# Transformer stack with self and cross attention on one core: query and key transfers issued per round instead of from one ordered queue

## The chip, the cores and the metric

The kernel runs on one core of a Trainium2 chip. The time is device microseconds (us) of one execution; the median of several executions counts. The engines are TensorE (PE: matrix products and, as PEld, loads of their stationary operand), VectorE (DVE), ScalarE (ACT), GpSimd (POOL) and SyncE (SP), whose queue issues nearly all DMA transfers here.

## The reference

Two layers; each has self attention, cross attention to a context of 1,601 rows, and a gated feed-forward part. There are 4 batches of 512 rows of width 320, and 20 heads of width 16.

```python
def _attn(x, ctx, wq, wk, wv, wo, bo, heads):
    ...
    sim = jnp.einsum('bhid,bhjd->bhij', q, k) * scale
    a = jax.nn.softmax(sim, axis=-1)
    out = jnp.einsum('bhij,bhjd->bhid', a, v)
    out = out.transpose(0, 2, 1, 3).reshape(b, n, heads * dh)
    return out @ wo + bo
...
h1 = _ln(x, n1_g, n1_b)
x = _attn(h1, h1, q1, k1, v1, o1_w, o1_b, heads) + x
h2 = _ln(x, n2_g, n2_b)
x = _attn(h2, context, q2, k2, v2, o2_w, o2_b, heads) + x
h3 = _ln(x, n3_g, n3_b)
proj = h3 @ ff_w1 + ff_b1
a, g = jnp.split(proj, 2, axis=-1)
ff = a * jax.nn.gelu(g, approximate=False) @ ff_w2 + ff_b2
return ff + x
```

## The kernel before

**Units.** Attention is cut into units of one batch and four heads: 20 self units, then 20 cross units, then four feed-forward units (one a batch), and the same for layer 1. The units are numbered through: 0 to 19 self, 20 to 39 cross, 40 to 43 feed-forward, 44 on for layer 1. A self unit has 4 chunks of 128 keys, a cross unit 13. The four heads lie in four strips of 32 rows, so that products of four heads can run on PE side by side.

**One chunk** (`main`, from L1117). For each head PE forms the scores `st` from keys and queries (L1128: two products with the two halves of the split queries, and a third with `nrows` and `ones`, which takes the row maximum off). ACT takes the exponentials (L1138), PE multiplies them with the values into `av` (L1152, one chunk late), ACT copies that to `vo` (L1168) and POOL adds it to `o` (L1169). Two *rounds* are counted a chunk.

**Pair products.** The row maxima of a coming unit are needed before its scores. They come from products `sps` of two heads each (L936), which DVE reduces to `nmax` or `pm` (L953). A self unit has 8 of them, a cross unit 26. `giver` (L1380) hands one a round to the chunk in hand, if a unit among the next two (or the first cross unit, which is marked early) has its data *at hand*, that is, three rounds after its reads were issued (`at_hand`, L1363). What is then still missing one round before the maxima are due is given as a lump behind the chunk's scores. Two chunks before a unit starts, `max_end` (L1000) splits and turns its maxima on DVE and sends them to the rows `nrows` by eight transfers (L1015) from SP.

**Queries and keys.** `add_proj` (L648) puts a unit's projections into the scheduler's chains: for a self unit `both` (L721 on PE, L737 on ACT, the split into `high` and `low` on POOL at L645), for a cross unit `keys_of_context` (L787) and `queries` (L759). The results go to DRAM (`kway`, `qway`, two buffers of each) and come back in another layout to `kT` and `q`. Each such step is a *move*, issued from SP at L690. A self unit has five: write the keys (2 transfers), write the queries (3), read the keys (1), read the two halves of the queries (1 and 1). A cross unit has eight. A unit's read waits for the unit three before it, whose buffers it takes (`unread`, `free`).

**The order.** `steps` (L400) runs once a chunk and picks, from the heads of the chains, the one that is due first; each step has a cost and a due round, and a running credit says how much may be done. The moves stand in a chain of their own, "slots", in the order in which the units were added; only its head may go, one move a round (`add_moves`, L819), and two rounds after the last move of its unit. If a unit is wanted whose moves have not all gone, `at_once` (L1367) issues them, with its projections if these are missing, on the spot.

Of the kernel before, what the change touches and what calls it, by code (L numbers as in the profile page):

```python
# [65 lines left out]
def kernel(ctx: ExitStack, tc: tile.TileContext, x, context, ws, out):  # L66
# [264 lines left out]
    chains = {n: deque() for n in ("divide", "project", "slots", "norm", "context", "early", "proj", "values")}  # L331
    clock = {"round": 0, "credit": 0.0, "lights": 0, "slots": 0, "tiles": None}
# [67 lines left out]
    def steps(beside, lights=1):  # L400


        tick()
        clock["lights"], clock["slots"] = lights, 1
# [233 lines left out]
    pending = {"q": 0, "k": 0}  # L638

    def by_rows(t):  # L640
        return t.rearrange("j h d n -> j (h d) n")
# [6 lines left out]
    def add_proj(u):  # L648
        chain = "early" if u.early else "proj"

        due = lead(u) - 9
# [30 lines left out]
        def move(pairs, then=None, what=None, may=yes):  # L682
# [13 lines left out]
            u.moves.append((f, yes if what else may))  # L696
            u.moving = clock["round"]

# [16 lines left out]
        def both(part):  # L715
# [29 lines left out]
            move([(to_q[:, 0], high[:GD]), (to_q[:, 1], low[:GD]), (to_q[:, 2], high[:GD])], what="q")  # L745
            move([(u.kT[:, u.k0 : u.k0 + N].bitcast(F32), by_rows(to_k))], may=free)
            read_queries(to_q)
# [31 lines left out]
        def keys_of_context():  # L779
# [27 lines left out]
            move([(full[:, :, i * HALF : (i + 1) * HALF], of[:, i, :, :HALF]) for i in range(2)], may=free)  # L807
            move([(to[:, 4 * QT :].rearrange("p (a w) -> p a w", a=4), of[:, 1, :, HALF:])], may=free)
# [10 lines left out]
        def add_moves(n, due):  # L819
            for _ in range(n):  # L820
                add(
                    "slots", 0.0, lambda: u.moves and u.moves.popleft()[0](), due,
                    lambda: u.moves[0][1]() if u.moves else u.when is not None,
                    lambda: clock["slots"] > 0 and clock["round"] >= u.moving + 2,
                )

        if not u.cross:
            for part in range(2):
                add(chain, (0.46,) * 3, lambda part=part: both(part), due - 2 + 2 * part, lambda part=part: part or way_free("q") and way_free("k"))
            add_moves(5, due)  # L830
        else:
            add(chain, 2.45, keys_of_context, keys_due, lambda: way_free("k"))
            add_moves(4, keys_due)
# [3 lines left out]
            add_moves(4, due)  # L837
# [378 lines left out]
    def add_norms(i):  # L1216

        while norms and norms[0].i <= i + (1 if norms[0].kind == "ff" else AHEAD + 1 if norms[0].early else 6):
# [3 lines left out]
            else:  # L1222
# [4 lines left out]
                due = lead(u) - 10  # L1227
# [139 lines left out]
    def at_once(v):  # L1367
# [7 lines left out]
        while v.moves:  # L1375
            f, may = v.moves.popleft()
            assert may()
            f()
# [97 lines left out]

    for i, u in enumerate(units):
# [44 lines left out]
```

## Time and profile before

| | |
|---|---|
| median of three executions | 4405.97 us (4396.28 to 4408.82) |
| profiled execution | 4397.83 us |
| its span, first to last instruction | 4396.0 us |
| mean granted clock of PE | 0.819 |
| PE busy | 3874.0 us (88%) |
| DVE, ACT, POOL busy | 2104.9, 1973.4, 1124.2 us |
| DMA, mean over the span | 51 GB/s |

An engine's busy time is the union of its instructions. The granted clock is the share of full speed at which PE was let run; at 0.5 every product takes twice its time. A row of the timeline gives start, length, engine, source line, operation, output <- inputs, shapes and a count of instructions merged; in brackets stands the idle time before it and what ended it. A row of a group gives busy time and mean ns of one, and after the bar the idle time before it. A row of waits gives the total, the number and the longest.

By the count of values products the stages of the profiled execution end at about 705 us (self, layer 0), 1960 us (cross, layer 0), 2296 us (feed-forward, and the first self unit of layer 1), 2908 us (self, layer 1), 4116 us (cross, layer 1).

### The profile page before, as it was taken

To read this page: it belongs to the slowest core of one execution; us is meant where nothing else is said; L and a number is where in the kernel's file an instruction comes from. 1 tells how busy PE (TensorE), PEld (TensorE's weight loads), DVE (VectorE), ACT (ScalarE), POOL (GpSimd) and SP (SyncE) were. 2 spreads that over 40 slices of the span, in tenths; PEclk is the share of its full clock that TensorE was granted. 3 is DMA by queue.
4 is the path that set the end of the run, shared out by engine and by line. 5 is a ranking of instruction groups with operands and counts; after the bars stand their busy time and mean duration, and the time that the engine had idled before them with its cause. 6 is when DMAs were issued, how large, how long until landed. Compare 5 with 4: busy or idle time off the path is not lost.

```text
span 4396.0 us, 82324 instructions
## 1 busy us (share of the span) xinstructions
PE 3874.0 (88%) x34290; PEld 1896.2 (43%) x34290; DVE 2104.9 (48%) x3113; ACT 1973.4 (45%) x3909; POOL 1124.2 (26%) x1222
## 2 busy tenths in 40 slices
PE   6778778899899999999988787788999899999999
PEld 3334344334434444545543333343344345445455
DVE  4434452524527776762234344535146376767321
ACT  2334334244255776771123333342443577777411
POOL 2222122122233344330111222221222344443200
PEclk7787687557678998999996877775577899999999
DMA  2221111110112122120012212111101121211100
GB/s 83 75 73 60 61 53 31 46 51 24 50 52 72 58 65 81 58 57 4 14 37 73 67 44 65 52 30 34 46 28 43 53 83 61 67 56 52 50 11 12
DMA packets 202224, 223.24 MB, mean 51 GB/s; under 512 B 63760, under 2 KB 143772, under 8 KB 201852
## 3 DMA queue, kind: packets, MB, share of 16 engines
q1 hardware_dynamic: 201468, 217.59, 16.4%
q8 instruction: 269, 4.41, 0.4%
q14 instruction: 103, 0.84, 0.1%
q10 hardware_dynamic: 176, 0.27, 0.0%
q0 software_dynamic: 208, 0.14, 0.0%
HBM read 119.55 MB, written 86.58 MB: 47 GB/s over the span
## 4 chain that ended last, share of the span: by engine, by line
PE 60%; DVE 14%; DMA 11%; ACT 5%; SPq 4%; issue 2%; POOL 2%; POOLq 0%; DVEq 0%; ACTq 0%
PE st L1128 19%; PE av L1152 16%; DVE pm L953 9%; PE fps L1258 6%; ACT pr L1138 4%; DMA qway<-high 4%; PE yps L1312 4%; DVE nmax L953 3%; DMA q<-qway 3%; DMA kway<-stages 3%; PE sps L936 3%; PE ops L1062 2%; PE kps L787 2%; PE vps L878 2%; SPq L690 2%
## 5 line engine op out<-in xcount | busy, mean ns | idle before, releaser
L1138 ACT ACTIVATE pr<-st 128x512 f32<-128x512 f32 (+1 forms) x2720 | 1404.2, 603 | 1098.2 <-PE st L1128 1052.5
L1169 POOL TENSOR_TENSOR o<-o,vo 128x512 f32<-128x512 f32 x576 | 736.3, 1278 | 2161.8 <-ACT vo L1168 2154.0
L1128 PE MATMUL st<-q,kT 32*128 32x512 f32 (+1 forms) x5440 | 1127.7, 523 | 142.9 <-ACT low L737 63.1
L953 DVE TENSOR_REDUCE pm<-sps 128x2 f32<-128x1024 f32 (+1 forms) x1142 | 1134.5, 1047 | 245.3 <-PE sps L936 211.9
L936 PE MATMUL sps<-kT,q 32*128 32x512 f32 x5120 | 1022.6, 547 | 194.5 <-DMA q<-qway 117.8
L1152 PE MATMUL av<-pr,vals 128*32 128x512 f32 (+1 forms) x5440 | 890.6, 727 | 122.2 <-ACT pr L1138 120.2
L1128 PEld LDWEIGHTS st<-q,kT 32*128 32x128 f32 (+1 forms) x5440 | 509.1, 207 | 885.9 <-ACT pr L1138 456.9
L936 PEld LDWEIGHTS sps<-kT,q 32*128 32x128 f32 x5120 | 460.8, 223 | 477.3 <-DVE pm L953 179.3
L953 DVE TENSOR_REDUCE nmax<-sps 128x1 f32<-128x512 f32 (+1 forms) x459 | 381.7, 894 | 565.9 <-PE sps L936 556.6
L1128 PE MATMUL st<-nrows,ones 2*128 2x512 f32 (+1 forms) x2720 | 603.9, 456 | 29.3 <-DMA nrows<-turned 26.6
L1168 ACT COPY vo<-av 128x512 f32<-128x512 f32 x576 | 347.1, 603 | 143.8 <-PE av L1152 141.7
L1128 PEld LDWEIGHTS st<-nrows,ones 2*128 2x128 f32 (+1 forms) x2720 | 329.5, 215 | 73.7 <-issue 24.0
L1152 PEld LDWEIGHTS av<-pr,vals 128*32 128x32 f32 (+1 forms) x5440 | 118.3, 116 | 436.0 <-ACT pr L1138 423.0
L1258 PE MATMUL fps<-hT,w 128*128 128x512 f32 x640 | 284.3, 597 | 0.6 <-DVE hid L1282 0.6
L1281 ACT ACTIVATE gl<-fps,b 128x512 f32<-128x512 f32 x80 | 50.6, 683 | 391.6 <-PE fps L1271 274.0
L1032 DVE STREAM_TRANSPOSE oturn<-o 128x512 f32<-128x512 f32 x80 | 56.3, 704 | 272.2 <-POOL o L1169 272.1
L1258 PEld LDWEIGHTS fps<-hT,w 128*128 128x128 f32 x640 | 118.8, 190 | 148.9 <-issue 144.0
L1282 DVE SCALAR_TENSOR_TENSOR hid<-fps,b,gl 128x512 f32<-128x512 f32 x80 | 56.4, 747 | 263.0 <-ACT gl L1281 263.0
L1312 PE MATMUL yps<-w,hid 128*128 128x320 f32 x640 | 175.3, 434 | 1.3 <-DVE nmax L953 1.3
L645 POOL CAST high<-low 128x256 fp32r<-128x256 f32 (+1 forms) x79 | 39.6, 501 | 491.0 <-ACT low L737 314.8
L1312 PEld LDWEIGHTS yps<-w,hid 128*128 128x128 f32 x640 | 120.7, 190 | 56.9 <-issue 6.1
L737 ACT ACTIVATE low<-qkps,scales 128x256 f32<-128x256 f32 x78 | 35.2, 472 | 243.9 <-DMA qway<-low 132.6
(86 smaller groups left out, 2560.0 us busy)
## 6 DMA issues: line engine op xcount, KB each, us to landing
q<-qway SPq DMA_DIRECT2D x160, 256.0 KB
kway<-stages SPq DMA_DIRECT2D x160, 224.0 KB
kT<-kway SPq DMA_DIRECT2D x80, 384.0 KB
kT<-kway SPq DMA_DIRECT2D x40, 256.0 KB
aT<-o SPq DMA_DIRECT2D x320, 32.0 KB
qway<-high SPq DMA_DIRECT2D x160, 64.0 KB
nrows<-turned SPq DMA_DIRECT2D x636, 2.0 KB
qway<-high SPq DMA_DIRECT2D x79, 128.0 KB
```

What stands on the lines that cost most here:

```text
L690: queue.dma_start(out=to, in_=of)
L787: nc.tensor.matmul(ps[i * GD : (i + 1) * GD, :w], lhsT=wk_q[rows, k, u.g * GD : (u.g + 1) * GD], rhs=first.kvT[rows, k, i * HALF : i * HAL ...
L878: nc.tensor.matmul(ps[:, :w], lhsT=u.kvT[rows, k, s * P : (s + 1) * P], rhs=wv_q[rows, k, h0 * DH : h1 * DH], start=(k == 0), stop=(k == K ...
L936: nc.tensor.matmul(ps, lhsT=u.q[j * SLOT : (j + 1) * SLOT, e, t * P : (t + 1) * P], rhs=u.kT[j * SLOT : (j + 1) * SLOT, u.k0 + s * 512 : u ...
L953: nc.vector.tensor_reduce(to[:, j : j + n], part, AX.X, ALU.max, negate=(ns == 1))
L1128: nc.tensor.matmul(st[:r, :], lhsT=ones[rows.start : rows.start + 2, :r] if e == 2 else u.keys(rows, c), rhs=u.rows[rows.start : rows.star ...
L1138: nc.scalar.activation(p[:r], st[:r], AF.Exp)
L1152: nc.tensor.matmul(ps[j * SLOT : (j + 1) * SLOT, :], lhsT=columns_of[:r, head : head + SLOT], rhs=pr.pop((c, j))[:r, :], start=True, stop= ...
L1168: nc.scalar.copy(vo, ps)
L1169: nc.gpsimd.tensor_tensor(u.o, u.o, vo, ALU.add)
L1258: nc.tensor.matmul(ps, lhsT=w1[:, k, i * FF + c * P : i * FF + (c + 1) * P], rhs=u.hT[:, k, :], start=ahead and k == 0, stop=not ahead and ...
L1312: nc.tensor.matmul(ps[:, :D], lhsT=hid[c][:, t * P : (t + 1) * P], rhs=w2[:, c, :], start=(c == 0), stop=(c == NHC - 1),)
```

## The change

The chain "slots" goes. A list `movers` holds the units that have moves left, and a new function `carry`, called once at the end of `steps`, goes through them in the order of the units and issues each unit's next moves as long as they may go, two rounds after that unit's last one, with room for three transfers a round. A self unit's reads of keys and queries become one move of three transfers, a cross unit's reads of full and remaining keys one, and its reads of the query halves one. A self unit's projections are added with unit `i + 4` in place of `i + 3` and are due 18 rounds ahead instead of 9, its normalisation 20 instead of 10.

```diff
-    chains = {n: deque() for n in ("divide", "project", "slots", "norm", "context", "early", "proj", "values")}
+    chains = {n: deque() for n in ("divide", "project", "norm", "context", "early", "proj", "values")}
...
-            clock["slots"] -= name == "slots"
         clock["tiles"] = None
+        carry()
...
     pending = {"q": 0, "k": 0}
+    movers = []
+
+    def carry():
+
+        room = 3
+        for u in sorted(movers, key=lambda u: u.i):
+            while u.moves and u.moves[0][1]() and clock["round"] >= u.moving + 2 and room > 0:
+                room -= u.moves[0][2]
+                u.moves.popleft()[0]()
+            if not u.moves:
+                movers.remove(u)
...
-        due = lead(u) - 9
+        due = lead(u) - (9 if u.cross else 18)
...
-            u.moves.append((f, yes if what else may))
+            u.moves.append((f, yes if what else may, len(pairs)))
             u.moving = clock["round"]
+            if u not in movers:
+                movers.append(u)
...
-        def read_queries(t):
-            for e in range(2):
-                move([(u.q[:, e].bitcast(F32), by_rows(t[:, e : e + 2]))], there if e else None, may=unread)
+        def read_queries(t, keys=[]):
+            reads = [(u.q[:, e].bitcast(F32), by_rows(t[:, e : e + 2])) for e in range(2)]
+            move(keys + reads, there, may=lambda: unread() and (u.cross or free()))
...
-            move([(u.kT[:, u.k0 : u.k0 + N].bitcast(F32), by_rows(to_k))], may=free)
-            read_queries(to_q)
+            read_queries(to_q, [(u.kT[:, u.k0 : u.k0 + N].bitcast(F32), by_rows(to_k))])
...
-        def add_moves(n, due):
-            for _ in range(n):
-                add(
-                    "slots", 0.0, lambda: u.moves and u.moves.popleft()[0](), due,
-                    lambda: u.moves[0][1]() if u.moves else u.when is not None,
-                    lambda: clock["slots"] > 0 and clock["round"] >= u.moving + 2,
-                )
...
-                due = lead(u) - 10
+                due = lead(u) - (10 if u.cross else 20)
...
+    add_proj(units[3])
     for i, u in enumerate(units):
...
-        for k in (3, AHEAD):
+        for k in (3, 4, AHEAD):
             v = units[i + k] if i + k < len(units) else None
-            if v is not None and v.kind != "ff" and v.early == (k == AHEAD):
+            if v is not None and v.kind != "ff" and k == (4 if not v.cross else AHEAD if v.early else 3):
                 add_proj(v)
```

In the order of the program the change shows on SP first. In the rows below `q_103` to `q_105` are the three query buffers, `kT_102` the keys of the self stage, and `kway`, `qway` the buffers in DRAM. Before, in layer 0's self stage, units 7 and 8 (queries to `q_104` and `q_105`) are issued in one run:

```order
L690 DMA kway_137<-high 4x16x512
L690 DMA kway_137<-low 4x16x512
L690 DMA qway_135<-high 4x16x512
L690 DMA qway_135<-low 4x16x512
L690 DMA qway_135<-high 4x16x512
L690 DMA kT_102<-kway_137 128x512
L690 DMA q_104<-qway_135 128x1x512 x2
L690 DMA kway_138<-high 4x16x512
L690 DMA kway_138<-low 4x16x512
```

After the change, the read of unit 8 and the writes of unit 9 on the same queue:

```order
L1017 DMA nrows_100<-turned 4x4x32 x8
L222 DMA w_117<-in_L_xattn_v_dram 32x6x320 x2
L1055 DMA aT<-o 16x512 x4
L701 DMA kT_102<-kway_138 128x512
L701 DMA q_105<-qway_136 128x1x512 x2
L222 DMA w_117<-in_L_xattn_v_dram 32x6x320
L701 DMA kway_137<-high 4x16x512
L701 DMA kway_137<-low 4x16x512
L222 DMA w_117<-in_L_xattn_v_dram 32x6x320
L701 DMA qway_135<-high 4x16x512
L701 DMA qway_135<-low 4x16x512
L701 DMA qway_135<-high 4x16x512
```

Writes and reads of one unit now stand apart, with other units' transfers between them. On PE, before, a chunk of unit 8 (scores from `q_105`) with pair products of units 9 (`q_103`) and 10 (`q_104`) and the projection of unit 10 (`qkps`) ahead of them:

```order
L1128 MATMUL st<-q_105,kT_102 128x512 x8
L1128 MATMUL st<-nrows_100,ones 128x512 x4
L936 MATMUL sps<-kT_102,q_103 128x512 x8
L1152 MATMUL av<-pr,vals 32x512 x4
L721 MATMUL qkps<-hT,wqk 128x256 x6
L936 MATMUL sps<-kT_102,q_103 128x512 x24
L936 MATMUL sps<-kT_102,q_104 128x512 x24
```

After, a chunk of unit 6 (scores from `q_103`), with pair products of unit 8 (`q_105`):

```order
L734 MATMUL qkps<-hT,wqk 128x256 x6
L1130 MATMUL st<-q_103,kT_102 128x512 x2
L938 MATMUL sps<-kT_102,q_105 128x512 x2
L1130 MATMUL st<-q_103,kT_102 128x512 x2
L938 MATMUL sps<-kT_102,q_105 128x512 x2
L1130 MATMUL st<-nrows_100,ones 128x512 x2
L1130 MATMUL st<-q_103,kT_102 128x512 x4
L938 MATMUL sps<-kT_102,q_105 128x512 x2
L1130 MATMUL st<-nrows_100,ones 128x512 x2
L938 MATMUL sps<-kT_102,q_105 128x512 x2
L1154 MATMUL av<-pr,vals 32x512 x4
```

The pair products stand between the scores instead of in a lump behind a projection. In the cross stage, before, unit 20 hands over to units 21 (`q_103`, `kT_443`) and 22 (`q_104`):

```order
L936 MATMUL sps<-kT_443,q_103 128x512 x8
L787 MATMUL kps<-ctxT,w_117 64x224 x48
L936 MATMUL sps<-kT_443,q_103 128x512 x8
L759 MATMUL qps<-hT,wq_114 32x256 x12
L936 MATMUL sps<-kT_443,q_103 128x512 x72
L964 MATMUL sps<-kT_443,q_103 128x66 x32
L936 MATMUL sps<-kT_102,q_104 128x512 x96
```

After, a chunk of unit 20 (`q_444`, `kT_442`) with pair products of unit 21:

```order
L1130 MATMUL st<-q_444,kT_442 128x512 x2
L938 MATMUL sps<-kT_443,q_103 128x512 x2
L1130 MATMUL st<-q_444,kT_442 128x512 x2
L938 MATMUL sps<-kT_443,q_103 128x512 x2
L1130 MATMUL st<-nrows_100,ones 128x512 x2
L1130 MATMUL st<-q_444,kT_442 128x512 x4
L938 MATMUL sps<-kT_443,q_103 128x512 x2
L1130 MATMUL st<-nrows_100,ones 128x512 x2
L938 MATMUL sps<-kT_443,q_103 128x512 x2
L1154 MATMUL av<-pr,vals 32x512 x4
```

The 25 rounds of pair products in one lump have become one round a chunk and a round now and then behind it.

More of the change, by code (lines that the diff above doesn't have):

```diff
@@ L403, in steps @@
         tick()
-        clock["lights"], clock["slots"] = lights, 1
+        clock["lights"] = lights
         clock["tiles"] = True if beside is None else None
@@ L744, in both @@
             move([(to_k[:, 0], high[GD:]), (to_k[:, 1], low[GD:])], what="q")
-            move([(to_q[:, 0], high[:GD]), (to_q[:, 1], low[:GD]), (to_q[:, 2], high[:GD])], what="q")
-            move([(u.kT[:, u.k0 : u.k0 + N].bitcast(F32), by_rows(to_k))], may=free)
-            read_queries(to_q)
+            move([(to_q[:, e], t[:GD]) for e, t in enumerate((high, low, high))], what="q")
+            read_queries(to_q, [(u.kT[:, u.k0 : u.k0 + N].bitcast(F32), by_rows(to_k))])
             u.keyed = True
@@ L806, in keys_of_context @@
             full = to[:, : 4 * QT].rearrange("p (a w) -> p a w", a=4)
-            move([(full[:, :, i * HALF : (i + 1) * HALF], of[:, i, :, :HALF]) for i in range(2)], may=free)
-            move([(to[:, 4 * QT :].rearrange("p (a w) -> p a w", a=4), of[:, 1, :, HALF:])], may=free)
+            reads = [(full[:, :, i * HALF : (i + 1) * HALF], of[:, i, :, :HALF]) for i in range(2)]
+            reads.append((to[:, 4 * QT :].rearrange("p (a w) -> p a w", a=4), of[:, 1, :, HALF:]))
+            move(reads, may=free)
             first.made["kv"] += 1
@@ L1375, in at_once @@
         while v.moves:
-            f, may = v.moves.popleft()
+            f, may, _ = v.moves.popleft()
             assert may()
```

5 lines of the change are left out of this document (1 added, 4 removed).

## The prediction

> **What bounds the kernel now.** I read the page first, its slices of TensorE (PE) and of its clock. A digit is a tenth; a slice is 110 us.
>
> ```profile
> PE   6778778899899999999988787788999899999999
> PEclk7787687557678998999996877775577899999999
> ```
>
> PE is the busiest engine. The first 13 slices (layer 0's self stage and the start of its cross stage) and slices 22 to 31 (the same places of layer 1) show it mostly at a low clock, and idle for a good part; elsewhere both are mostly at 9. Next I read stages: the line of the values product (L1152, 8 records a chunk, so 32 a self unit and 104 a cross unit) counts the units in a stretch. Columns: stretch, length, PE busy (records), weight loads, granted clock, DMA share, GB/s.
>
> ```profile
> core 0: us, PE busy (x) PEld busy (x), PEclk, DMA share, GB/s
> 104.00:705.00 601.00, 99.22 (x576) 12.57 (x576) 0.76 0.20 60
> 705.00:1405.00 700.00, 156.94 (x836) 18.60 (x832) 0.69 0.16 47
> 1405.00:1893.00 488.00, 148.66 (x1044) 20.85 (x1040) 0.94 0.22 66
> 2296.00:2908.00 612.00, 113.31 (x608) 13.52 (x608) 0.74 0.18 55
> 2908.00:3525.00 617.00, 134.39 (x732) 16.23 (x728) 0.69 0.14 41
> 3525.00:4048.00 523.00, 158.45 (x1148) 22.76 (x1144) 0.96 0.22 66
> ```
>
> So 18 self units take 601 us (33.4 each) in layer 0 and 19 take 612 (32.2) in layer 1. The first 8 cross units of layer 0 take 700 (87.5 each) where the next 10 take 488 (48.8); in layer 1 the first 7 take 617 (88.1) and the next 11 take 523 (47.5). The same work costs almost twice as much in one place as in another, and the clock goes with it. The timeline of PE shows why, at one of the places where a unit is handed over late:
>
> ```profile
> 168.27 2.87 PE L721 MATMUL qkps<-hT,wqk 112*128 112x256 f32 x12
> 171.06 0.50 PE L1128 MATMUL st<-q,kT 32*128 32x512 f32 x2
> 176.75 1.58 PE L1128 MATMUL st<-q,kT 32*128 32x512 f32 x6 [5.18 <-ACT low L737]
> 177.71 1.05 PE L1128 MATMUL st<-nrows,ones 2*128 2x512 f32 x4
> 181.88 0.80 PE L936 MATMUL sps<-kT,q 32*128 32x512 f32 x4 [3.12 <-DMA q<-qway]
> 184.67 0.80 PE L936 MATMUL sps<-kT,q 32*128 32x512 f32 x4 [1.99 <-DMA q<-qway]
> ...
> 195.86 7.06 PE L936 MATMUL sps<-kT,q 32*128 32x512 f32 x24 [0.41 <-DVE nmax L953]
> ```
>
> The scheduler finds units 3 and 4 unread when their maxima are due, so it issues their writes and reads at once, projects unit 4 on the spot, and PE waits for the round trip through DRAM (5.2, 3.1, 2.0 us); then it does their pair products in one lump instead of between the scores. The cross stage does the same with lumps of 25 rounds:
>
> ```profile
> 772.42 0.80 PE L936 MATMUL sps<-kT,q 32*128 32x512 f32 x4 [3.70 <-DMA q<-qway]
> ...
> 810.88 26.36 PE L936 MATMUL sps<-kT,q 32*128 32x512 f32 x94
> ...
> 837.76 1.39 PE L1128 MATMUL st<-q,kT 32*128 32x512 f32 x2 [0.51 <-DVE pm L953]
> ```
>
> From 772.42 to 837.76 PE works at little but two units' pair products, 65 us. A round of a lump is two pairs, 8 products: 26.36 us for 94 is 2.24 us a round. Between scores the same products are nearly free; rows of a steady cross unit:
>
> ```profile
> 3674.47 0.50 PE L1128 MATMUL st<-q,kT 32*128 32x512 f32 x2
> ...
> 3677.18 0.50 PE L1128 MATMUL st<-q,kT 32*128 32x512 f32 x2
> ...
> 3680.01 0.50 PE L1128 MATMUL st<-q,kT 32*128 32x512 f32 x2
> ```
>
> A chunk with scores, one round of pair products and the values product begins every 2.7 to 2.8 us there.
>
> **The change, part by part.** By the order, the head-of-line wait is gone. Before, self units from 3 on (odd ones unread, even ones not even projected) and cross units 1 to 6 or so are forced; after, one unit a layer (18) is. The products L936 stand between scores nearly everywhere.
>
> *Cross stage.* The chunk is that of the steady windows, so I price the first units as the later ones of their layer. Layer 0: 8 x 48.8 = 390 for 700, **-310**. Layer 1: 7 x 47.5 = 333 for 617, **-284**. Bounds: 46 a unit (the waits of the steady windows go too) to 54 (one such lump of 65 us stays in every ten units): -33 and +95 us for 15 units.
>
> *Self stage.* No row of before shows a smooth self unit, so I build one. Four chunks of 2.8 are 11.2. Its own work, from the groups of lines in 2296 to 2908 (19 units):
>
> ```profile
> L721 PE MATMUL qkps<-hT,wqk 112*128 112x256 f32 (+1 forms) x192 | 58.4, 463 | 0.0
> L860 PE MATMUL vps<-wv,hT 112*32 112x192 f32 (+3 forms) x600 | 29.7, 344 | 0.7 <-DVE nmax L953 0.7
> L1062 PE MATMUL ops<-wo,aT 112*32 112x160 f32 (+1 forms) x576 | 26.8, 331 | 2.2 <-DVE nmax L953 1.9 <-DVE pm L953 0.3
> L499 PE MATMUL hps<-ident,hn 128*112 128x128 f32 (+1 forms) x36 | 5.0, 279 | 0.0
> L787 PE MATMUL kps<-ctxT,w 32*64 32x224 f32 x192 | 5.6, 353 | 0.5 <-DVE pm L953 0.5
> ```
>
> 125.5 / 19 = 6.6, so 17.8 us of PE. Next, the wait that the change creates. A self unit may be read only when the unit three before it is scored, and its first pair product stands one and a half chunks later: 1.1 (values product) + 2.8 + 1.4 + the share of other work (two quarters of 6.6) = 8.6 us. What the read takes, from SyncE (SP) and the PE rows above:
>
> ```profile
> 173.57 0.34 SPq L690 DMA_DIRECT2D kT<-kway  x1
> 176.17 1.79 SPq L690 DMA_DIRECT2D q<-qway  x2
> ```
>
> From the key issue, 181.88 - 173.57 = 8.3 us to the first half of the queries and 11.1 to the second, in one run of three transfers as the change makes it. So PE waits about 2.5 us a unit: nothing at the least, the whole 8.3 if the other work stands elsewhere. The third term is the maxima's round trip, also on SP, behind more transfers than before:
>
> ```profile
> PE st L1128 <- DMA nrows<-turned: 16.9, 7, 5.5
> ```
>
> That is the steady cross window, 16.9 / 11 = 1.5 us a unit; I take 1.5 (bounds 0 and 5.5). Sum 21.8, taken as **22** (19.5 to 28). VectorE (DVE) and ScalarE (ACT) hold less, 14.0 and 12.1 us a unit (266.88 and 229.59 over 19):
>
> ```profile
> 2296.00:2908.00 612.00, 486.96 (x4000) 237.57 (x3992) 266.88 (x453) 229.59 (x459) 129.88 (x153) 0.74 0.18 55
> ```
>
> The lumps that stay: the order leaves one of 7 rounds for the first cross unit and one of 7 rounds for units 17 and 18, with unit 18 still forced. 14 x 2.24 = 31, and 5 for unit 18's round trip, which four rounds cover in part: 36 a layer. Layer 0: 18 x 22 + 36 = 432 for 601, **-169**. Layer 1: 19 x 22 + 36 = 454 for 612, **-158**.
>
> *Smaller parts.* SP issues the same transfers but two. A self read waits at SP's head for its unit's writes and for the scores of the unit three before; behind it stand the next unit's writes and, a chunk or two later, the eight row transfers of the maxima (L1015) that PE needs, which is the third term above. Those scores are issued ahead of the read, so the head is short. Self projections and norms come a unit earlier, still between scores; their wait for buffers has the same slack. By the order, 40 of 5,120 pair products are missing: unit 16 of each layer closes its maxima before its own pairs, so its exponent's shift is what the buffer held; 10 pairs at under 1.2 us, counted as nothing. Feed-forward and the last cross units keep their rows.
>
> Sum: 310 + 284 + 169 + 158 = 921. The profiled execution took 4397.83 us with a span of 4396.0; 4397.83 - 921 = 3477, put at **3475**. It lies 8 us (0.2%) under the median, inside the runs; I shift nothing.
>
> **The rivals.**
>
> *The transfers set the self stage's pace.* The rows of sizes and the stretch in which only q and k are read:
>
> ```profile
> q<-qway SPq DMA_DIRECT2D x160, 256.0 KB
> qway<-high SPq DMA_DIRECT2D x79, 128.0 KB
> ...
> 178.60:184.20 5.60, 0.96 (x5) 0.32 (x4) 0.00 (x0) 1.84 (x4) 0.89 (x1) 0.50 0.25 91
> 791.00:958.00 167.00, 156.95 (x778) 60.00 (x786) 54.87 (x81) 66.70 (x126) 30.35 (x25) 0.50 0.11 32
> ```
>
> The first stretch runs at 91 GB/s with a DMA share of 0.25, four engines of sixteen. A self unit's 5 writes and 3 reads are 1408 KB, 15.8 us at that rate. That is below 22, but it queues reads behind writes. If that adds 6 us a unit: 37 x 6 = 222, **3700**. The Trainium skill, DMA: Bandwidth & Descriptors, "Why a DMA increments its semaphore by 16 and not by 1", says that a transfer uses the largest number of engines up to 16 that divides the slowest dimension of both sides, the lowest-numbered ones. With four heads slowest that is always the same four engines, and the trace's 0.25 agrees; by it alone the 15.8 us would be a floor and the sum unchanged.
>
> *Slower: the clock sticks at half.* The second stretch above (791 to 958) has PE busy 157 of 167 us and still a clock of 0.50, so being busy alone does not bring the clock back. If the newly smooth stages stayed there: a self unit 2 x 17.8 + 4 = 39.6, +17.6 x 37 = 651; a cross unit 47.5 x 0.96 / 0.50 = 91, +43.7 x 15 = 655; together 1306, **4783**. It turns slower than before once 921 of these 1306 come, seven tenths. Against: that stretch is scores without pair products, and the windows with the interleaved chunk, which the order now shows throughout, hold 0.94 and 0.96. The Trainium skill, TensorE: Matmul & The Clock Gate, "What's actually happening", has full clock after one busy window of about 3.4 us. The 167 us disagree and the measurement decides; by the rule this rival would have no chance and the sum would stay.
>
> *The change doesn't do what it says in the self stage*: data still arrive as late as before, by waits instead of lumps, and only the cross stage gains: 3477 + 169 + 158 = **3804**.
>
> *Better than built*: 19.5 a self unit, lumps at 20, cross at 46: 93 + 32 + 33 less, **3320**.
>
> **How the numbers follow.** Forecast (3320 to 3600) 0.66; transfers set the pace 0.19; below 3320 0.06; no gain in the self stage 0.05; slower 0.03; gains and a partly stuck clock cancel 0.01. A measurement of this kernel tells about 0.3% from no change. Range 3320 to 3720: it leaves out 0.15 and a rest for wider transfers. Faster 0.96, same 0.01, slower 0.03.
>
> **What would show it.** Cross units at 47 to 50 us from the first on; self units near 22; clock above 0.9 in both; waits of PE for q<-qway many and near 2.5 us, not 10; L936 at 5,080. Wrong if the self windows keep a clock near 0.75, if PE waits for the maxima in every self unit, or if the cross stage still shows lumps beyond the first unit.

## The result, and the profile after

| | before | after |
|---|---|---|
| median of four executions | 4402.58 us (4396.28 to 4408.82) | 3533.68 us (3530.80 to 3542.65) |
| ratio, with its 95% interval | | 0.803 [0.8011, 0.8049] |
| profiled execution, its span | 4397.83, 4396.0 us | 3533.73, 3531.6 us |
| PE busy | 3874.0 us | 3194.2 us |
| mean granted clock | 0.819 | 0.925 |

The forecast was 3475 us in a range of 3320 to 3720; the time lies in the range, 59 us above the forecast. Of the ten executions of the experiment `dense_fill` below, one took 6971.29 us; it counts in the median given there and not in the ratio.

From the profile's page after the change, the slices of PE and of its clock, now 88 us each:

```profile
PE   6887888899999989999997888889999999999999
PEclk7788968999999989999998988789999999999999
```

Of the places with a low clock only the start and the two self stages are left (slices 1 to 7 and 22 to 27, but for slice 15 with an 8). The hollows at the start of both cross stages are gone. The busy times split the gain: PE works 3874.0 - 3194.2 = 680 us less for the same products but for the 40 pair products left out (34,250 records for 34,290), at a higher mean clock and beside each other, and it stands idle only 337 us for 522. So four fifths of the 864 us by which the span shrank are not waits that went, but the same products done in less time.

The windows after, cut by the same counts of values products (L1154 now); columns as in the prediction:

```profile
core 0: us, PE busy (x) PEld busy (x), PEclk, DMA share, GB/s
114.00:577.00 463.00, 95.32 (x576) 12.30 (x576) 0.83 0.27 79
577.00:979.00 402.00, 116.64 (x832) 16.66 (x832) 0.94 0.25 74
979.00:1463.00 484.00, 145.45 (x1040) 20.71 (x1040) 0.95 0.23 69
1859.00:2325.00 466.00, 96.93 (x608) 12.79 (x608) 0.83 0.25 76
2325.00:2668.00 343.00, 101.31 (x732) 14.53 (x728) 0.96 0.23 67
2668.00:3184.00 516.00, 155.66 (x1148) 22.66 (x1144) 0.97 0.23 67
```

Set beside the prediction's windows, stage by stage (us):

| stage | before | forecast | after | after - before |
|---|---|---|---|---|
| start, two units | 104 | 104 | 114 | +10 |
| self, layer 0, 18 units | 601 | 432 | 463 | -138 |
| cross, layer 0, first 8 | 700 | 390 | 402 | -298 |
| cross, layer 0, next 10 | 488 | 488 | 484 | -4 |
| last 2, feed-forward, first self unit | 403 | 403 | 396 | -7 |
| self, layer 1, 19 units | 612 | 454 | 466 | -146 |
| cross, layer 1, first 7 | 617 | 333 | 343 | -274 |
| cross, layer 1, next 11 | 523 | 523 | 516 | -7 |
| rest | 348 | 348 | 348 | 0 |

The last column adds up to -864, the change of the span. The forecast's sum was -921; the 57 us by which it was too large are +31 and +12 in the self stages, +12 and +10 in the first cross units, +10 at the start, and -18 elsewhere.

What a self unit waits for now is seen in layer 1, in the timelines of SP and of PE after the change:

```profile
1906.24 0.53 SPq L701 DMA_DIRECT2D kT<-kway  x1
1906.82 1.21 SPq L701 DMA_DIRECT2D q<-qway  x2
...
1913.38 0.80 PE L938 MATMUL sps<-kT,q 32*128 32x512 f32 x2 [4.30 <-DMA q<-qway]
...
1916.34 0.79 PE L938 MATMUL sps<-kT,q 32*128 32x512 f32 x2 [2.16 <-DMA q<-qway]
```

The read goes out when the unit three before is scored. PE has its next pair product standing in its order well before the data land, and waits 4.30 us for the first half of the queries and 2.16 for the second, 10.1 us after the keys' issue. The waits of PE for these reads, in the self windows of layer 0 and of layer 1 and over the whole run (total, number, longest):

```profile
PE sps L938 <- DMA q<-qway: 53.9, 21, 6.5
...
PE sps L938 <- DMA q<-qway: 58.2, 24, 5.5
...
PE sps L938 <- DMA q<-qway: 153.9, 62, 15.6
```

That is 3.0 and 3.1 us a unit. Each is a short wait, but there is one or more at nearly every unit; before, the whole run had 117.8 us of them in 55 waits. And the two lumps of seven rounds that the prediction left in each layer are still there, in units 15 and 16. The two windows below are those units, in layer 0 and layer 1. The rows of PE are of layer 0: the longest run of the first lump and the scores behind it, and products at the head of the second lump, which wait for their unit's read:

```profile
428.60:509.50 80.90, 11.95 (x64) 1.44 (x64) 0.73 0.18 56
2176.90:2257.20 80.30, 12.56 (x64) 1.48 (x64) 0.70 0.19 58
...
440.93 9.39 PE L938 MATMUL sps<-kT,q 32*128 32x512 f32 x32 [0.41 <-DVE pm L955]
450.83 1.39 PE L1130 MATMUL st<-q,kT 32*128 32x512 f32 x2 [0.51 <-DVE pm L955]
...
474.88 0.80 PE L938 MATMUL sps<-kT,q 32*128 32x512 f32 x4 [2.25 <-DMA q<-qway]
```

### The profile page after: what moved, and what is told of

It reads as the page before. It is cut to its first block, busy times and chain, and to the rows that moved or that the text cites. A ratio compares the mean times of both kernels' runs of the same rounds, so it can differ in the third digit from the quotient of the medians.

```text
span 3531.6 us, 81984 instructions
## 1 busy us (share of the span) xinstructions
PE 3194.2 (90%) x34250; PEld 1675.7 (47%) x34250; DVE 2092.8 (59%) x2835; ACT 1966.7 (56%) x3909; POOL 1127.0 (32%) x1223
## 4 chain that ended last, share of the span: by engine, by line
PE 64%; DMA 14%; DVE 7%; SPq 7%; ACT 3%; issue 3%; POOL 2%; ACTq 0%; DVEq 0%; POOLq 0%
PE st L1130 18%; PE av L1154 15%; PE fps L1260 8%; DMA q<-qway 8%; PE yps L1314 5%; DVE pm L955 3%; PE ops L1064 3%; PE sps L938 3%; SPq L1017 3%; ACT pr L1140 3%; DMA kway<-stages 3%; PE vps L880 2%; PE kps L799 2%; PE qkps L734 2%; SPq L701 2%
## 5 line engine op out<-in xcount | busy, mean ns | idle before, releaser
L938 PE MATMUL sps<-kT,q 32*128 32x512 f32 x5080 | 947.8, 464 | 197.3 <-DMA q<-qway 153.9
L1130 PE MATMUL st<-q,kT 32*128 32x512 f32 (+1 forms) x5440 | 1033.7, 455 | 31.2 <-ACT stages L808 10.4
L1154 PE MATMUL av<-pr,vals 128*32 128x512 f32 (+1 forms) x5440 | 791.5, 651 | 41.3 <-ACT pr L1140 35.9
L1130 PE MATMUL st<-nrows,ones 2*128 2x512 f32 (+1 forms) x2720 | 637.5, 416 | 48.6 <-DMA nrows<-turned 47.2
L955 DVE TENSOR_REDUCE nmax<-sps 128x2 f32<-128x1024 f32 (+1 forms) x347 | 370.7, 1105 | 358.2 <-PE sps L938 346.8
L938 PEld LDWEIGHTS sps<-kT,q 32*128 32x128 f32 x5080 | 417.4, 195 | 281.1 <-issue 117.4
L1154 PEld LDWEIGHTS av<-pr,vals 128*32 128x32 f32 (+1 forms) x5440 | 113.5, 111 | 311.7 <-ACT pr L1140 288.9
L656 POOL CAST high<-low 128x512 fp32r<-128x512 f32 (+1 forms) x79 | 39.6, 501 | 291.5 <-ACT low L750 231.8
L1064 PEld LDWEIGHTS ops<-wo,aT 112*32 112x32 f32 (+1 forms) x3072 | 100.3, 114 | 68.1 <-issue 31.0
L1064 PE MATMUL ops<-wo,aT 112*32 112x160 f32 (+1 forms) x3072 | 131.9, 312 | 0.6 <-DVE pm L955 0.6
```

Source lines behind the costliest of these rows:

```text
L938: nc.tensor.matmul(ps, lhsT=u.q[j * SLOT : (j + 1) * SLOT, e, t * P : (t + 1) * P], rhs=u.kT[j * SLOT : (j + 1) * SLOT, u.k0 + s * 512 : u ...
L955: nc.vector.tensor_reduce(to[:, j : j + n], part, AX.X, ALU.max, negate=(ns == 1))
L1064: nc.tensor.matmul(ps[f : f + m, : D // 2], lhsT=aT[:n, k, t * P + f : t * P + f + m], rhs=wo[:n, k, cols], start=(k == 0), stop=(k == 2),)
L1130: nc.tensor.matmul(st[:r, :], lhsT=ones[rows.start : rows.start + 2, :r] if e == 2 else u.keys(rows, c), rhs=u.rows[rows.start : rows.star ...
L1154: nc.tensor.matmul(ps[j * SLOT : (j + 1) * SLOT, :], lhsT=columns_of[:r, head : head + SLOT], rhs=pr.pop((c, j))[:r, :], start=True, stop= ...
```

## The experiments

The theory was the prediction's: the gain comes from moves that no longer wait for the head of one queue; the clock comes back because pair products stand between scores; what a self unit still costs over a smooth one is the read's way through DRAM. The rivals: it is the earlier projections that do it; the low clock has another cause; transfers, not their lateness, set the self stage's pace.

### Which half of the change: `queue_only` and `early_only`

`queue_only` is the kernel after with the self projections where they were:

```diff
-        due = lead(u) - (9 if u.cross else 18)
+        due = lead(u) - 9
...
-                due = lead(u) - (10 if u.cross else 20)
+                due = lead(u) - 10
...
-    add_proj(units[3])
...
-        for k in (3, 4, AHEAD):
+        for k in (3, AHEAD):
...
-            if v is not None and v.kind != "ff" and k == (4 if not v.cross else AHEAD if v.early else 3):
+            if v is not None and v.kind != "ff" and v.early == (k == AHEAD):
```

> The changed kernel without its earlier self projections and norms (9 and 10 rounds ahead, added three units ahead, as before); the per-round issue and the single read stay. Theory (the ordered queue's head held everything back): nearly all of the gain stays, 3500 to 3620 us, the first cross units at 47 to 50 us each, no lump over 6 rounds. Rival (the projections came too late, the queue did not matter): little gain, over 4100 us, self units still above 30 us.

`early_only` is the kernel before with these lines the other way round, its one queue kept.

> The kernel before with only the self projections and norms made a unit sooner; the ordered queue and the separate reads stay. Theory (ordered queue): no gain worth the name, 4330 to 4450 us, the lumps of 7 and 25 rounds stay. Rival (lateness of the projections): most of the gain, under 3800 us.

Measured: `queue_only` 3530.76 us, ratio to before 0.8013 [0.7987, 0.8038]; `early_only` 4334.81 us, 0.9829 [0.9804, 0.9854]. The windows of `queue_only` (self, cross, self, cross) and then of `early_only`, in the same four stages:

```profile
116.00:558.00 442.00, 95.21 (x580) 12.27 (x576) 0.84 0.27 83
558.00:961.00 403.00, 116.37 (x832) 16.62 (x832) 0.94 0.25 73
1861.00:2321.00 460.00, 98.59 (x608) 12.84 (x608) 0.87 0.26 79
2321.00:2680.00 359.00, 101.31 (x732) 14.49 (x728) 0.94 0.21 65
```

```profile
105.00:715.00 610.00, 105.12 (x576) 12.75 (x576) 0.75 0.19 60
715.00:1417.00 702.00, 154.91 (x836) 18.59 (x832) 0.69 0.16 47
2295.00:2904.00 609.00, 108.98 (x608) 13.37 (x608) 0.76 0.18 56
2904.00:3477.00 573.00, 130.06 (x732) 15.96 (x728) 0.72 0.15 44
...
822.90 26.36 PE L936 MATMUL sps<-kT,q 32*128 32x512 f32 x94
```

The issue per round, with a unit's reads in one move, gives the whole gain without the earlier projections (what the one move adds is asked in `three_moves`), and it forms all 5,120 pair products. With earlier projections alone the lump of 94 products stays to the hundredth of a microsecond, and of these four windows only layer 1's first cross units gain (617 to 573). In the kernel after, the earlier projections buy nothing that is measured in the whole time. By stage they do move time: without them the self windows are 21 and 6 us shorter, layer 1's first seven cross units 16 us longer and layer 0's next ten 13 us longer, which about cancels. The first cross units of `queue_only`, 50.4 and 51.3 us each, lie just above the 47 to 50 expected. What the earlier projections are worth when reads are short comes below.

### Is it the read's length: `double_reads` and `wide_reads`

`double_reads` reads both query halves twice, the same data to the same place:

```diff
-            move(keys + reads, there, may=lambda: unread() and (u.cross or free()))
+            move(keys + reads + reads, there, may=lambda: unread() and (u.cross or free()))
```

> The changed kernel with both halves of the queries read twice, one read behind the other, so 512 KB more a unit on the same four engines (about 5.7 us at the 91 GB/s of a read alone). Theory (the read's transfer time is what PE waits for in the self stage): self units take 4 to 6 us more each, cross units hardly anything, the time rises by 150 to 250 us to 3680 to 3790. Rival (the wait is not the transfer): under 40 us more.

Measured: 3807.75 us, ratio 0.8642 [0.8622, 0.8661], 274 us above the kernel after. Its self window of layer 1 and the waits in it:

```profile
2005.00:2567.00 562.00, 101.49 (x608) 13.00 (x608) 0.77 0.25 80
...
PE sps L938 <- DMA q<-qway: 131.7, 30, 10.2
```

That is 96 us more in 19 units, 5.1 us each, of which 73.5 are longer waits (131.7 for 58.2); the clock falls from 0.83 to 0.77 with them. The rate hardly rises (80 GB/s for 76, at a DMA share of 0.25 in both): the added bytes lengthen the unit. The whole is more than the 150 to 250 us expected: 96 and 81 us lie in the self stages as expected, but most of the rest lies in the cross stages, which were expected to lose hardly anything and whose queries are read twice too (363 us for 343 in layer 1's first seven units).

`wide_reads` makes the reads shorter with the same bytes read: the queries lie in DRAM in the order in which they are read, so that a read is 128 rows on both sides where it was four heads of 32. The queries' low half is written twice for it (four writes a unit for three), in the cross stage too, and keys are read as 128 rows.

```diff
-    q_way = [dram.tile([HG, 3, DH, N], F32, name=f"qway{i}") for i in range(2)]
+    q_way = [dram.tile([2, HG, 2, DH, N], F32, name=f"qway{i}") for i in range(2)]
...
-            reads = [(u.q[:, e].bitcast(F32), by_rows(t[:, e : e + 2])) for e in range(2)]
+            reads = [(u.q[:, e].bitcast(F32), t[e].rearrange("j h d n -> (j h d) n")) for e in range(2)]
...
-            move([(to_q[:, e], t[:GD]) for e, t in enumerate((high, low, high))], what="q")
+            move([(to_q[e // 2, :, e % 2], t[:GD]) for e, t in enumerate((high, low, low, high))], what="q")
-            read_queries(to_q, [(u.kT[:, u.k0 : u.k0 + N].bitcast(F32), by_rows(to_k))])
+            read_queries(to_q, [(u.kT[:, u.k0 : u.k0 + N].bitcast(F32), to_k.rearrange("j h d n -> (j h d) n"))])
...
-                move([(to_q[:, e, :, cols], t) for e, t in enumerate((hi, lo, hi))], what="q")
+                move([(to_q[e // 2, :, e % 2, :, cols], t) for e, t in enumerate((hi, lo, lo, hi))], what="q")
```

> The changed kernel with the self units' reads, and all reads of queries, laid out in DRAM as 128 equal rows, so that a read's slowest dimension is 128 and not 4; the queries take one write of 128 KB more a unit for it. Theory (PE waits in each self unit for the reads to be transferred by four engines): waits for q<-qway in the two self windows fall from 112 us to under 40, the clock there rises above 0.88, the time falls by 60 to 130 us to 3405 to 3475. Rival (the wait is issue and latency, or the writes in front): waits stay above 80 us, time within 25 us of 3534 or longer.

Measured: 3443.70 us, ratio 0.7812 [0.7797, 0.7827], 90 us below the kernel after, with more bytes written. Its timelines in layer 1, one unit later than those shown above, its two self windows, and the waits in them:

```profile
1876.42 0.53 SPq L701 DMA_DIRECT2D kT<-kway  x1
1877.00 0.90 SPq L701 DMA_DIRECT2D q<-qway  x2
...
1880.05 0.49 PE L938 MATMUL sps<-kT,q 32*128 32x512 f32 x2 [0.61 <-DMA q<-qway]
...
1881.47 0.50 PE L938 MATMUL sps<-kT,q 32*128 32x512 f32 x2 [0.92 <-DMA q<-qway]
```

```profile
107.00:547.00 440.00, 93.84 (x580) 12.13 (x576) 0.85 0.30 89
1817.00:2237.00 420.00, 91.65 (x608) 12.49 (x608) 0.88 0.30 91
...
PE sps L938 <- DMA q<-qway: 21.7, 15, 4.4
...
PE sps L938 <- DMA q<-qway: 20.5, 14, 3.6
```

From the keys' issue to the product of the second half it is 5.0 us here; at the unit shown above it was 10.1, and at that same unit `wide_reads` has 5.9. The waits in the self windows go from 112 us to 42, and the windows from 929 us to 860, about as much. (The waits were expected under 40 and the clock above 0.88; both fall just short.) In the stretch of the read, after the change (first) and in `wide_reads` (second), the DMA share and the rate show why:

```profile
1906.20:1916.30 10.10, 3.68 (x33) 1.30 (x26) 2.98 (x3) 4.27 (x9) 2.00 (x2) 0.80 0.49 131
```

```profile
1877.50:1881.40 3.90, 2.44 (x22) 1.04 (x18) 3.06 (x6) 3.06 (x7) 1.27 (x1) 1.00 0.71 226
```

Both stretches hold other units' transfers too (writes, and in the first also weights), so 0.49 is more than the reads' own share. The second begins 1.1 us behind the keys' issue; taken from the issue on, 1876.4 to 1881.5, it has a share of 0.60 and 186 GB/s. The one read of 256 KB of queries whose landing the trace times, from POOL's queue at the start, took 5.7 us after the change and 2.8 us in `wide_reads`. The rule in the Trainium skill, DMA: Bandwidth & Descriptors, "Why a DMA increments its semaphore by 16 and not by 1" (as many engines, up to 16, as divide the slowest dimension of both sides), gives four engines for four heads and 16 for 128 rows; the trace agrees, with 0.25 in the prediction's stretch, where only such reads ran, and 0.71 here, which four engines of sixteen could not reach. The writes, whose four heads give four engines by the same rule, were left as they are.

`wide_queue` then puts `wide_reads` and `queue_only` together, to ask again what the earlier projections are worth.

> The changed kernel with the reads spread over 128 rows and without the earlier self projections and norms. Theory (the earlier projections add nothing once the queue is gone, as without the spread): within 30 us of the 3444 us with them. Rival (they were paid back by the slow reads alone): over 3480 us.

Measured: 3489.78 us, ratio 0.7950 [0.7914, 0.7985], 46 us above `wide_reads`, and above the rival's 3480. So the earlier projections are worth something only once the read is short. Part of the 46 us is that `wide_queue` forms all 5,120 pair products and `wide_reads` 5,080 (about 13 us by `urgent` below). By stage of the profiled executions, which lie 37 us apart, 28 us are in layer 1's self window (448 us for 420), 14 in the later cross units of layer 0 and 7 in its first, 9 come back in layer 1's later cross units, and layer 0's self window has none (439 us in both). That the projection is next in line behind the read would explain it, but layer 0's self window does not bear it out; the cause is not shown.

### The wait moved instead of shortened: `hand4` and `three_moves`

`hand4` counts a unit as at hand four rounds after its read's issue, not three, so that PE's order has the first pair product later:

```diff
-        return v.when is not None and clock["round"] >= v.when + 3
+        return v.when is not None and clock["round"] >= v.when + 4
```

> The changed kernel, but a unit's pair products may start four rounds after its reads were issued, not three. Theory (PE waits because the first pair product stands too close behind the read): the waits for q<-qway in the two self windows fall from 112 us to under 75, and since the first cross unit no longer takes the rounds of unit 16, the two lumps of 7 rounds a layer shrink: time 3430 to 3510. Rival (what is not given in the rounds comes back as a lump of one round a unit at 2.2 us, 35 units): time within 25 us of 3534.

Measured: 3470.48 us, ratio 0.7876 [0.7849, 0.7902], 63 us below the kernel after. The group of pair products, and the self windows:

```profile
L938 PE MATMUL sps<-kT,q 32*128 32x512 f32 x5120 | 952.6, 459 | 107.0 <-DMA q<-qway 73.3 <-DVE pm L955 17.8 <-ACT low L750 5.6
...
111.00:547.00 436.00, 91.13 (x580) 11.99 (x576) 0.86 0.28 85
1831.00:2251.00 420.00, 93.83 (x612) 12.58 (x608) 0.89 0.28 85
```

The waits for queries fall from 153.9 us to 73.3 though the reads keep their bytes and their layout: half of the waiting came from an order that asked one round too soon. That is not the whole gain. The lumps of units 15 and 16 shrink too, as expected (no run of L938 in the self windows is longer than 12): the two units take 68.0 us in layer 0 and 60.9 in layer 1 for 80.9 and 80.3, which is 32 of the 73 us by which the self windows are shorter. The pair products are complete here (5,120), so this is not bought with work left out.

`three_moves` splits the self read again into three moves, as before, each two rounds behind the other, and a cross unit's query read into two:

```diff
-            move(keys + reads, there, may=lambda: unread() and (u.cross or free()))
+            for pair in keys:
+                move([pair], may=free)
+            for e in range(2):
+                move([reads[e]], there if e else None, may=unread)
```

> The changed kernel with a self unit's read cut again into three moves (keys, first half, second half of the queries), and a cross unit's query read into two, each two rounds apart; the per-round issue and the earlier projections stay. Theory (the reads of a unit must go together because each move costs two rounds of the nine there are): a self unit is at hand four rounds later, half its pair products come in lumps, time 3560 to 3700. Rival (the merge only saves SP issues): within 25 us of 3534.

Measured: 3583.84 us, ratio 0.8139 [0.8124, 0.8155], 50 us above. Layer 0's self window, with all engines (PE, weight loads, DVE, ACT, POOL), in the kernel after and then in `three_moves`; under the latter its waits for queries in that window, and one run of its pair products (L941 there):

```profile
114.00:577.00 463.00, 372.49 (x3846) 198.41 (x3850) 254.37 (x391) 219.55 (x439) 129.65 (x149) 0.83 0.27 79
```

```profile
116.00:618.00 502.00, 407.79 (x3874) 212.87 (x3877) 263.89 (x423) 220.35 (x438) 129.69 (x149) 0.79 0.24 72
...
PE sps L941 <- DMA q<-qway: 38.2, 10, 12.9
...
549.09 2.08 PE L941 MATMUL sps<-kT,q 32*128 32x512 f32 x16
```

A later read shows as *less* waiting (38.2 us for 53.9) in a longer window: the pair products come late and in runs of 10 to 16 behind the scores, and the time is in PE's busy column, 35 us more at a lower clock. Who reads only the waits would have taken this kernel for the better one. In layer 1 the same edit moves time the same way but loses none: its self window has 36 us less of these waits (21.9 us for 58.2) and 20 us more in PE's busy column, and takes 464 us for 466. Layer 0's 39 us are most of the 50; why only layer 0 loses was not separated.

### The pair products left out: `urgent`

The kernel after forms 5,080 of 5,120 pair products. `urgent` gives a lump to the unit whose maxima are about to close, which forms all:

```diff
+                if urgent is not None and left(urgent):
+                    v = urgent
```

> The changed kernel, but a lump that is owed to a unit whose maxima are due goes to that unit and not to the first cross unit, so that unit 16 of each layer forms all its 8 pair products ahead of its maxima (the changed kernel forms 3, and these behind them): 5,120 products L936/L938 in place of 5,080. Theory (the left-out products are worth next to nothing, the lumps stay as long): time within 25 us of 3534. Rival (the left-out products hid a wait for unit 16's read): 25 to 60 us more, with a wait for q<-qway of over 8 us in unit 15.

Measured: 3546.36 us, ratio 0.8059 [0.8041, 0.8077], 13 us more, with all 5,120. By the two ratios and their intervals that is 1 to 24 of the 869 us; the place of the lump changes with it, so the left-out work alone is not parted from that.

### What holds the clock at half: `dense_fill` and `thin_fill`

Both are the kernel before, with four needless products in each of the 267 chunks that have no pair products between their scores; the one on 128 rows and 128 columns of the array, the other on 32 rows of it:

```diff
+    def keep_busy():
+        ps = ps_m.tile([P, 2, 512], F32, tag="m", name="busyps")
+        for i in range(4):
+            nc.tensor.matmul(
+                ps[:, 0, i * P : (i + 1) * P], lhsT=ident[:P, :], rhs=ident[:P, :], start=True, stop=True
+            )
...
+                if len(products) == HG and not extra:
+                    keep_busy()
```

(`thin_fill` has `ident[:SLOT, :]`, 32 rows, in both operands.)

> The kernel before with four needless products of 128 rows by 128 columns (a constant with itself, result unread) added to each of the 267 chunks that have scores and no pair products. Theory (such a chunk leaves most of PE's rows idle, and that is why the clock sticks at 0.50 there although PE is busy; work that fills the rows frees it): the second cross unit of each layer, 59.9 us at 0.50 before, has a clock above 0.85 and takes under 56 us in spite of the added work; the whole time lies between 4250 and 4420 us. Rival (the clock follows the idle waits only, or time busy): that unit stays at 0.50 and takes 67 us or more; the whole time is 100 us or more longer.

> The same number of needless products, at the same places and as long, but of 32 rows instead of 128. Theory (filled rows free the clock, busy time does not): the second cross unit stays at 0.50 and takes 67 to 75 us, the whole time is 100 us or more longer than before. Rival (busy time counts, whatever the rows): the same as with 128 rows.

Measured: `dense_fill` 4393.85 us, ratio 0.9984 [0.9961, 1.0007]; `thin_fill` 4506.41 us, 1.0244 [1.0213, 1.0275]. The second cross unit of layers 0 and 1, whose chunks hold scores (32 rows) and values products (128 rows by 32 columns) and no pair products, in the kernel before, in `dense_fill` and in `thin_fill`; for each of the latter two a row of the fillers of one chunk (four products, two records each):

```profile
854.30:914.10 59.80, 25.16 (x104) 2.63 (x104) 0.50 0.06 16
3058.40:3118.20 59.80, 25.15 (x104) 2.63 (x104) 0.50 0.02 3
```

```profile
874.90:926.60 51.70, 14.68 (x104) 2.09 (x104) 0.93 0.05 14
3056.10:3105.40 49.30, 13.84 (x106) 2.04 (x104) 1.00 0.02 4
...
890.29 1.16 PE L356 MATMUL busyps<-ident 128*128 128x128 f32 x8
```

```profile
873.10:945.00 71.90, 25.13 (x104) 2.61 (x104) 0.50 0.04 10
3132.10:3204.00 71.90, 25.14 (x104) 2.61 (x104) 0.50 0.01 3
...
891.38 1.90 PE L356 MATMUL busyps<-ident 32*128 32x128 f32 x8
```

With *more* work, on the full array, the unit gets 8 and 10 us shorter, since the clock goes from 0.50 to 0.93 and 1.00; with the same number of products on a quarter of its rows it gets 12 us longer and the clock does not move. PE is busy for 93% of the unit before, 93% and 92% in `dense_fill` and 99% in `thin_fill`. So it is how much of the array the products fill that the clock follows in this unit, not how busy PE is. Over the whole kernel the higher clock and the added work cancel (0.998). The Trainium skill, TensorE: Matmul & The Clock Gate, "What's actually happening", has a busy window of about 3.4 us bring full speed; 59.8 us at 0.50, with PE busy for 55.6 of them, disagree, and the measurement decides. The score chunk of the kernel after has pair products between its scores, and in the cross windows, where they stand in nearly every chunk, the clock is 0.94 to 0.97 without needless work; that they do it by filling further strips of rows at the same time fits both runs, but was not measured apart.

### Both improvements together: `wide_hand4`

`wide_reads` and `hand4` in one kernel.

> The reads spread over 128 rows and the four rounds together. Theory (both act on the same wait, so the second adds only what the lumps of units 15 and 16 give): waits for q<-qway under 20 us in the self windows, time 3380 to 3435. Rival (the wait is gone already and the single rounds behind the chunks cost): 3440 or more.

Measured: 3415.92 us (3408.79 to 3424.73), ratio 0.7766 [0.7745, 0.7787], the fastest of all. The group of pair products:

```profile
L938 PE MATMUL sps<-kT,q 32*128 32x512 f32 x5120 | 941.9, 456 | 62.7 <-DMA q<-qway 29.3 <-DVE pm L955 17.1 <-DVE nmax L955 6.2
```

Alone the two gave 90 and 63 us, together 118: in part they remove the same wait, of which 29.3 us are left of 153.9. The mean clock rises to 0.946 with it.

## Why the prediction was right, point by point

**What bounds the kernel, and that it is the queue's head.** Right, and shown: `queue_only` brings all of it, `three_moves`, without the merged self read, all but 50 us, and `early_only`, which keeps the queue, keeps the lumps and 98% of the time.

**Cross stage at the steady price, 390 and 333.** Right to about 3%: 402 and 343, that is 50.3 and 49.0 us a unit for 48.8 and 47.5, inside the bounds of 46 to 54. The clock is 0.94 and 0.96, as in the windows from which the price was taken. That the clock would follow the interleaved pair products was argued from windows only; `dense_fill` and `thin_fill` show that it can be had by filling the array and not by keeping PE busy.

**The lumps that stay, 36 a layer.** Right: units 15 and 16 took 80.9 and 80.3 us, 37 and 36 above two units at 22.

**The self unit built at 22 us.** The mechanism was right, the size too small; this is the term that was mis-sized. Without units 15 and 16 it is (463 + 466 - 161) / 33 = 23.3 us, within the bounds of 19.5 to 28. Its parts over these 33 units: the read wait, priced 2.5, is 3.2 (105.8 us). The maxima's round trip, priced 1.5, shows there once, with 4.3 us; as a wait for the maxima that term was about nothing, but all of PE's other idle time together comes to 1.5, so here the sum was helped by luck. PE's busy time, priced at 17.8 with the small waits inside a chunk, is 18.5 (612.0 us). Chunks were priced at 2.8 us from windows with a clock near 0.95. The stretches ahead of units 15 and 16 have 0.86 and 0.87, those behind them 0.80, and with the two lumps the self windows have 0.83, so the sign "clock above 0.9 in both" did not come. The clock of the self windows is lower where they wait more: 0.77 and 0.78 with the reads doubled, 0.85 and 0.88 with wide reads, 0.86 and 0.89 with `hand4`. Waits are not all of it: the last three self units, at 0.80, wait little for queries (5.7 and 1.7 us in all) and have only 32 of the pair products L938, against 424 and 444 in the 13 and 14 units ahead of the lumps. The prediction named the clock in a rival, all or nothing, but put no price on a part of it.

**Omitted pair products at nothing.** Nearly right: about 13 us, in `urgent`, and `queue_only` forms all of them in the same time as the kernel after.

**Not priced**: 10 us at the start, which `queue_only` has (116) and `early_only` has not (105), so it belongs to the issue per round. The start is 135 us with the reads doubled and 107 with wide reads, so the reads have a part in it; more is not known. The later cross units and feed-forward gave 18 us back, without which the forecast would have been 75 us off.

**The rivals.** *Transfers set the pace*: not as a floor, since a self unit at 23.3 us stays above the 15.8 us of its transfers, but `wide_reads` shows that reads at the rate of the narrow layout cost 90 us of what is left, 69 of them in the self windows, by waits. *The clock sticks*: it did not in the cross stages, and in the self stages a part stayed, 0.83. The stretch from which this rival was argued, 791 to 958, was misread: it is not scores without pair products, since its first 46 us are mostly the lumps of pair products that the prediction's own rows show (810.88, 94 of them). The clean case is the unit at 854.30 above, and it has 0.50 too, so the argument holds. *No gain in the self stage*: out, 138 and 146 us.

**What stays open.** Whether wider writes would give more, and what the maxima's wait of 44.0 us, the largest left in `wide_hand4`, would cost to remove: not tried. Nor what the 46 us of `wide_queue` and the clock of 0.80 in the last three self units come from. By which count of rows, columns and time the clock is given was not measured, only that four full products a chunk sufficed here and four on 32 rows did not.

## What to carry to other kernels

When transfers with different conditions share one ordered chain, ask which of them the head holds up: issuing each when its own condition holds was worth a fifth of the time here, because the work that waited came back as lumps, and lumps cost twice, in order and in clock. Price a stage from a window with the same mixture of work *and the same waits*, since the clock was lower where PE waited more. And read a read's latency off the issue row and the first consumer: lay the source out as the destination's rows, and set the point at which the order first asks for the data by that latency.

## What the runs showed of the hardware that was not expected

- The granted clock followed the filling of the array here, not PE's busy time: 0.50 for whole units of scores and values products, 0.93 and 1.00 with four products on all 128 rows a chunk added, 0.50 still with four on 32 rows (51.7, 49.3 and 71.9 us a unit for 59.8). In these units more work took less time.
- The layout of a read in DRAM about halved its latency at the same bytes: from 10.1 to 5.9 us at one unit, and 5.0 at the next, from the keys' issue to the second half's use, with 131 GB/s in the stretch of the read before and 186 after.
- Reading a unit's 512 KB of queries twice lengthened a self unit by 5.1 us, with the DMA share still at 0.25 of 16 engines: a mean share far from full was no sign that transfers had room.
